# Turning the adjacency matrix of a graph network's second layer from int32 into bf16 during the first layer

## The chip, the cores and the metric

The kernel runs on one core of a Trainium2 chip. The metric is device time in microseconds (us) of one execution. The core's engines are called PE (matrix products), DVE (vector work), ACT (activations and copies), POOL (here almost only indirect DMAs) and SP (here only a queue that issues DMAs). Each runs its own instructions in the order in which they stand in its queue.

## The reference, cut to what matters

Four graph layers follow one another on 3327 nodes with 256 features each. All read one adjacency matrix `adj` of 3327 x 3327 int32, which holds zeros and ones; about 1% of it is ones. Each layer ends in a residual and a layer norm.

```python
def layer0(x, adj):              # score of an edge needs all 256 channels
    s, t = x @ Wsrc.T + bsrc, x @ Wtgt.T + btgt
    score = einsum('ijc,c->ij', leaky_relu(s[:, None, :] + t[None, :, :]), a)
    return softmax(where(adj != 0, score, -inf), 1) @ t
def layer1(x, adj):              # score is a sum of two numbers
    h = x @ W.T
    e = leaky_relu((h @ a1)[:, None] + (h @ a2)[None, :])
    return softmax(where(adj == 0, -1e9, e), 1) @ h
for layer in (layer0, layer1, layer2, layer3):
    x = layernorm(x + layer(x, adj))
```

Layers 2 and 3 are dense like layer 1; layer 3 has four heads, twice.

## The kernel before

Nodes come in 26 tiles of 128 rows (the last has 127).

**Layer 0** (`sparse0`) is sparse. It sorts the rows of four sets of 4, 7, 9 and 6 tiles by degree, makes a list of neighbours for each row and gathers the neighbours' rows from a table in device memory. A piece of this work is a *part*: up to four neighbours of all 128 rows of a tile, 237 parts in all. For a part POOL issues one indirect DMA a neighbour (L926, into buffer `g`), DVE scores it (L946 and L952), and once the scores of the whole tile are known, ACT multiplies each gathered row by its weight (L1028) and PE adds it up (L1031). There are 22 buffers `g`, so the gathers of part q wait until PE is done with part q - 22. The emitting loop at L1370 goes through the parts q in order. At each q it emits the steps that `due[q]` holds, the gathers of part q + 8, and the scoring of part q. Since the whole of layer 0 is under a manual schedule, what is emitted first comes first in each engine's queue. Between the parts, `neighbours` makes the lists of the next set: SP loads 512 KB pieces of `adj` (`adj_i`, three buffers), ACT turns them into bf16 (L553), PE and DVE search them.

`at_step(q, what)` puts a step at part q. Parts 39, 102 and 182 begin the sets 1, 2 and 3. While set 3 runs, layer 1 already does the share of its work that needs only the first 11 tiles (`KNOWN`): `ask_early`, `weigh_early` and `add_early` go through 44 pairs, loading int32 pieces of `adj_t`, the transposed matrix, into `at_f`, and leave bf16 copies of them in `at_d`, a buffer in device memory.

**Layer 1** (`one_head` with `l1`) multiplies, for each block of 4 to 6 target tiles, all 26 source tiles j. For each j it needs a strip of `adj_t`. `ask` loads it as int32 (`at_i`, from a pool of eight buffers with the tag `e`), DVE forms the weights `e` from it (`weigh`, L1728), and PE multiplies (L1845). `adjacent` also makes a bf16 copy on ACT (L1755), in a buffer `at` of a pool of three, and sends it to `at_d` through ACT's queue, for the layers behind.

```python
            if (j, b) not in asked:
                ask(j, b)
            at_i = asked.pop((j, b))
            nc.scalar.copy(at[:pn, :w], at_i[:pn, :w])
            copy_rows(nc.scalar, at_d[j * P : j * P + pn, c0:c1], at[:pn, :w])
            return at_i
```

The blocks of layer 1 (`blocks1`) have 5, 6, 4, 5 and 6 tiles and are worked on in `order1`: tiles 11 to 14 first, then 0 to 4, 5 to 10, 15 to 19, 20 to 25. The first block runs while the last set of layer 0 is normed and projected, a step of that after each j. Its loads of `at_i` are asked for three j ahead. The blocks of the tiles 0 to 10 skip the sources j below 11 and add the early sums (L1854).

**Layers 2 and 3** read strips of `at_d` into the three buffers `at`. Every one of these layers takes its features from tiles `feat` in on-chip memory. A second path (`dense0` and all layers anew, under `tc.If(again > 0)`) is for inputs that the sparse lists can't hold; it isn't taken with these inputs.

Of the kernel before, what the change touches and what calls it, by code (L numbers as in the profile page):

```python
# [8 lines left out]
F32 = mybir.dt.float32  # L9
BF16 = mybir.dt.bfloat16  # L10
I32 = mybir.dt.int32
# [8 lines left out]
P = 128  # L20
BANK = 512
# [11 lines left out]
SETS = (4, 7, 9, 6)  # L33
# [10 lines left out]
ROW = 260  # L44
# [6 lines left out]
def gat_stack(  # L51
# [29 lines left out]
    nc = tc.nc  # L81
    n, dim = x.shape
    nt = -(-n // P)
    kc = dim // P
# [4 lines left out]
    def rows_of(it):  # L89
        return min(P, n - it * P)  # L90
# [14 lines left out]
    at_d = dram.tile([nt * P, n], BF16, name="at_d")  # L105
# [15 lines left out]
    KNOWN = sum(SETS[:-2])  # L121
    blocks1 = []
    for lo, hi in ((0, KNOWN), (KNOWN, EARLY), (EARLY, nt)):
        count = -(-(hi - lo) // 6)
        ends = [lo + (hi - lo) * c // count for c in range(count + 1)]
        blocks1 += [list(range(a, b)) for a, b in zip(ends, ends[1:])]
    order1 = sorted(range(len(blocks1)), key=lambda b: (blocks1[b][0] != KNOWN, b))
    rate1_d = [
# [11 lines left out]
    def copy_rows(engine, dst, src):  # L140

        rows = dst.shape[0]
        whole = rows // 16 * 16
        for lo, hi in ((0, whole), (whole, rows)):
            if lo < hi:
                engine.dma_start(dst[lo:hi], src[lo:hi])
# [90 lines left out]
    blocks = [list(range(f, f + s)) for f, s in zip(firsts, sizes)]  # L237
# [3 lines left out]
    def cols_of(block):  # L241
        return block[0] * P, min(n, (block[-1] + 1) * P)
# [45 lines left out]
    def sparse0(lost):  # L288
        GROUP, TURNS, LEAD, SPREAD = 4, 22, 8, 8
        starts = [sum(SETS[:s]) for s in range(len(SETS))]  # L290
        with ExitStack() as s0:
            find = s0.enter_context(tc.tile_pool(name="s_find", bufs=2))
# [18 lines left out]
            def cuts_of(kt):  # L311

                ends = list(range(0, kt, GROUP)) + [kt]
                if kt % GROUP == 1:
                    ends[-2] -= 1
                return list(zip(ends, ends[1:]))
# [18 lines left out]
                )  # L335
                copy_rows(nc.sync, adj_i[:pn, : hi - lo], adj[it * P : it * P + pn, lo:hi])

            w_tgt = find.tile([P, kc, ROW], F32, name="w_tgt0", bufs=1)
            nc.scalar.dma_start(w_tgt[:, :, :dim], w_tgt_t.rearrange("(c p) f -> p c f", p=P))
            a_row = find.tile([P, dim], F32, name="a_row", bufs=1)  # L340
# [815 lines left out]
            def project_next(it):  # L1156
# [12 lines left out]
                for b, block in enumerate(blocks1):  # L1169
                    if it == block[-1]:  # L1170
# [6 lines left out]
                        nc.scalar.copy(row[:t], m[:t])  # L1177
                        nc.sync.dma_start(rate1_d[b][:, :], row[:t])

            trios = [  # L1180
                list(range(lo, min(lo + 3, block[-1] + 1)))
                for block in blocks1 if block[-1] < KNOWN
# [68 lines left out]
            first = neighbours(0)  # L1251
# [25 lines left out]
            ends, begins = {}, {}  # L1277
# [9 lines left out]
            def at_step(q, what, *args):  # L1287
                due.setdefault(q, []).append(lambda: what(*args))
# [17 lines left out]
            for q, key in ends.items():  # L1306
                count = len(cuts_of(seats[key]))
# [21 lines left out]
            for s in range(len(SETS) - 1):  # L1329
# [16 lines left out]
                at += 1  # L1346
            at_step(at, add_early, len(pairs1) - 1)
            at_step(at + 1, keep_early, len(pairs1) - 1)
            def keep_targets(s):
                lo, hi = starts[s] * P, min(n, (starts[s] + SETS[s]) * P)  # L1350
                copy_rows(nc.sync, own_d[s][: hi - lo, AT_TGT:], table_d[1 + lo : 1 + hi, :])
# [6 lines left out]
            for s in range(1, len(SETS)):  # L1358
                at = begins[s] - LEAD - 2
# [234 lines left out]
    def layers(rs, early=0, rest=None):  # L1594
# [145 lines left out]
            at_i = asked[j, b] = edges.tile([P, wide], I32, tag="e", name="at_i", bufs=8)  # L1740
            copy_rows(nc.sync, at_i[:pn, : c1 - c0], adj_t[j * P : j * P + pn, c0:c1])

        def adjacent(j, b, first=False):

            pn = rows_of(j)
            c0, c1 = cols_of((blocks1 if first else blocks)[b])
            w = c1 - c0
            at = links.tile([P, wide], BF16, tag="at", name="at")
            if not first:
                copy_rows(nc.sync, at[:pn, :w], at_d[j * P : j * P + pn, c0:c1])  # L1750
                return at
            if (j, b) not in asked:
# [68 lines left out]
        def one_head(layer, make, banks_next):  # L1821
# [1 line left out]
            folds, ready, used = [], {}, 0  # L1823

            def fetched(j, b):
                at = adjacent(j, b, layer is l1)
                return at, layer.weigh(j, b, at, 0) if layer.leaky else None

            for turn_b, b in enumerate(layer.order):
                block, first = layer.blocks[b], turn_b == 0  # L1830
# [5 lines left out]
                for j in range(skip, nt):  # L1836
                    pj = rows_of(j)
                    work_until(lambda: layer.feat[j] is not None)
                    at, e = ready.pop(j) if j in ready else fetched(j, b)
                    for s, it in enumerate(block):  # L1840
                        pn = rows_of(it)
                        for part in range(1 if layer.leaky else 3):
                            f = layer.feat[j] if layer.leaky else layer.feat[j][:, part, :]
                            a = e if layer.leaky else at
                            nc.tensor.matmul(  # L1845
                                accs[s][:pn, : dim + 1],
                                a[:pj, s * P : s * P + pn],
                                f[:pj, : dim + 1],
                                start=(j == skip and part == 0),
                                stop=(j == nt - 1 and (layer.leaky or part == 2)),  # L1850
                            )
                    if skip and j == skip + LATER:
                        for acc, y in zip(accs, parts):
                            nc.tensor.matmul(  # L1854
                                acc[:, : dim + 1], ident, y, start=False, stop=False
                            )
                    if layer is l1 and first:
                        work_off(2 if j > 10 else 1)
                        if j + 3 < nt:
                            ask(j + 3, b)  # L1860
                        fetch([j + 3])
                        if j > early and late:
                            l1.load_rates(late.pop(0))
                    elif j >= skip + LATER:
                        work_off()
                    if first and j in make:
                        made.append(make[j]())
                        folds += [(j + 4 + i, step) for i, step in enumerate(made[-1].fold())]
                    while folds and folds[0][0] <= j:
                        folds.pop(0)[1]()  # L1870
# [8 lines left out]
                for s, it in enumerate(block):  # L1879
                    pn = rows_of(it)  # L1880
# [258 lines left out]
        def load_heads(w, a):  # L2139
# [21 lines left out]
        l1 = Layer(  # L2161
            "l1", "f", 1, True, None, rate_d=rate1_d
        )
# [25 lines left out]

        if early:  # L2190
            l1.load_rates(late.pop(0), nc.sync)
        for j in range(3):
            ask(j, order1[0])
        fetch(range(3))
        if rest is not None:
# [109 lines left out]
```

## Time and profile before

| | us |
|---|---|
| median of 5 runs | 2906.27 (2897.23 to 2908.82) |
| the profiled execution: time / span of the core | 2908.21 / 2906.3 |
| PE busy | 2317.1 (80%) |
| DVE busy | 2128.0 (73%) |
| POOL busy | 990.4 (34%) |
| ACT busy | 866.0 (30%) |
| data read / written | 333.91 MB / 47.67 MB |

The profile is of one execution. Busy shares are means over stages that have different limits: POOL is busy from the start to about 1330 us, which is layer 0, and nearly idle after it. Layer 1 lies between about 1349 and 1660 us, layer 2 between 1660 and 1970 us, and layer 3 behind that. Lines of a timeline show the start, the time in us, the engine, the line and the operation; square brackets hold the idle time before it and what ended that. Lines of waits show the total in us, how many waits, and the longest.

### The profile page before, as it was taken

How to read it: one execution, taken by the hardware profiler on the slowest of the kernel's cores; microseconds unless marked ns; L12 is line 12 of the kernel's file. 1: busy time of each engine (PE TensorE's matmuls, PEld its weight loads, DVE VectorE, ACT ScalarE, POOL GpSimd, SP SyncE). 2: the span in 40 equal slices, each digit the busy share in tenths (PEclk: the TensorE clock that was granted, in tenths of full speed). 3: DMA queues.
4: the chain of work that ended last, by engine and by line, in shares of the span. 5: the costliest groups of instructions: out<-in, count | busy, mean ns of one | idle time of the engine just before them, and what ended most of it. 6: DMA issues, size and time to landing. Idle time of an engine off the chain costs nothing.

```text
span 2906.3 us, 47736 instructions
## 1 busy us (share of the span) xinstructions
PE 2317.1 (80%) x16764; PEld 1545.2 (53%) x16764; DVE 2128.0 (73%) x5634; ACT 866.0 (30%) x2441; POOL 990.4 (34%) x1059
## 2 busy tenths in 40 slices
PE   7466667555552665767899999999999999999997
PEld 4234435433442444645778888863656667534332
DVE  7799799968872856655455421158999999899997
ACT  4145445443432533544344211111011110111111
POOL 2676777777777777772000000000000000000000
PEclk9577778767776887889999999999999999999998
DMA  7795665555544457766767533331222222212211
GB/s 244 205 266 149 184 188 158 141 142 148 161 115 110 125 162 192 205 178 167 217 179 206 159 93 107 105 90 45 76 82 61 76 79 66 71 43 63 60 45 49
DMA packets 207558, 378.52 MB, mean 130 GB/s; under 512 B 38410, under 2 KB 148080, under 8 KB 206288
## 3 DMA queue, kind: packets, MB, share of 16 engines
q1 hardware_dynamic: 119416, 186.29, 22.6%
q0 software_dynamic: 50768, 154.31, 19.2%
q10 hardware_dynamic: 37128, 34.79, 3.6%
q8 instruction: 137, 2.24, 0.3%
q14 instruction: 109, 0.89, 0.1%
HBM read 333.91 MB, written 47.67 MB: 131 GB/s over the span
## 4 chain that ended last, share of the span: by engine, by line
PE 57%; DVE 15%; POOL 10%; issue 8%; DMA 7%; ACT 3%; ACTq 0%; SPq 0%; DVEq 0%; POOLq 0%
PE acc L1913 18%; PE acc L1845 14%; PE acc L1921 9%; PE acc L1031 9%; POOL g L926 8%; DMA g<-table_d,lst 3%; DVE y L952 3%; DVE e L1728 3%; PE misc L1653 3%; DVE y L946 2%; DVE cand L589 2%; ACT g L1028 1%; DMA at<-at_d 1%; PE early L1234 1%; DVE cand L599 1%
## 5 line engine op out<-in xcount | busy, mean ns | idle before, releaser
L926 POOL DMA_INDIRECT g<-table_d,lst x894 | 851.9, 953 | 275.9 <-issue 234.8
L1728 DVE SCALAR_TENSOR_TENSOR e<-rate,feat,at 128x896 f32<-128x896 f32 (+4 forms) x832 | 843.4, 1078 | 59.3 <-PE acc L1921 47.8
L1913 PE MATMUL acc<-e,feat 128*32 128x384 f32 (+2 forms) x6656 | 691.4, 514 | 2.9 <-DVE e L1728 1.5
L1031 PE MATMUL acc<-g,ident 128*128 128x256 f32 x1766 | 482.6, 429 | 67.4 <-ACT g L1028 46.3
L1913 PEld LDWEIGHTS acc<-e,feat 128*32 128x32 f32 x6656 | 306.8, 110 | 295.2 <-issue 157.4
L1031 PEld LDWEIGHTS acc<-g,ident 128*128 128x128 f32 x1766 | 376.9, 218 | 156.8 <-ACT g L1028 61.5
L1921 PE MATMUL acc<-e,feat 128*32 128x384 f32 (+3 forms) x3328 | 383.5, 512 | 0.0
L1028 ACT ACTIVATE g<-g,w 128x256 f32<-128x256 f32 x883 | 367.5, 495 | 15.0 <-ACT at L1217 10.6
L946 DVE TENSOR_TENSOR y<-g,minus_ps 128x1028 f32<-128x1028 f32 (+2 forms) x233 | 273.3, 1173 | 113.5 <-DMA g<-table_d,lst 106.7
L952 DVE SCALAR_TENSOR_TENSOR y<-y,a_ps 128x257 f32<-128x257 f32 x894 | 324.6, 419 | 14.5 <-PE a_ps L788 2.2
L1845 PE MATMUL acc<-feat,e 128*128 128x257 f32 (+1 forms) x1110 | 255.6, 386 | 16.9 <-DVE e L1728 13.2
L1845 PE MATMUL acc<-feat,at 128*128 128x257 bf16 (+2 forms) x2028 | 241.1, 276 | 9.8 <-DMA at<-at_d 9.2
L1845 PEld LDWEIGHTS acc<-feat,e 128*128 128x128 f32 (+1 forms) x1110 | 210.5, 192 | 51.8 <-DVE e L1728 15.2
L1921 PEld LDWEIGHTS acc<-e,feat 128*32 128x32 f32 (+1 forms) x3328 | 162.0, 110 | 131.0 <-issue 88.8
L1845 PEld LDWEIGHTS <-at 128*128 128x128 bf16 (+2 forms) x2028 | 200.3, 100 | 45.3 <-DMA at<-at_d 10.2
L563 PE MATMUL v<-code,leads 65*128 65x512 bf16 (+1 forms) x182 | 80.0, 440 | 143.5 <-DVE cand L589 100.3
L589 DVE MAX8 cand<-v 128x8 f32<-128x104 f32 (+2 forms) x858 | 157.6, 259 | 3.0 <-PE v L566 3.0
L1706 POOL DMA_DIRECT2D rate3b_d<-rate_rows x4 | 2.1, 520 | 449.8 <-ACT rate_rows L1705 449.8
L1728 DVE SCALAR_TENSOR_TENSOR e<-rate,feat,at_i 128x640 f32<-128x640 f32 (+4 forms) x108 | 95.8, 899 | 77.2 <-DMA at_i<-in_adj_t_dram 25.9
L1031 PE MATMUL acc<-own_of,ident 128*128 128x256 f32 x52 | 29.0, 659 | 136.7 <-ACT own_of L1028 85.6
L2099 POOL TENSOR_TENSOR rstds<-rstds,minus_half 128x7 f32<-128x7 f32 (+1 forms) x4 | 7.6, 1905 | 382.7 <-DVE rstds L2098 382.7
L261 POOL TENSOR_TENSOR rstds<-rstds,minus_half 128x6 f32<-128x6 f32 (+3 forms) x9 | 12.4, 1381 | 359.1 <-DVE rstds L260 359.1
(259 smaller groups left out, 2075.8 us busy)
## 6 DMA issues: line engine op xcount, KB each, us to landing
adj_i<-in_adj_dram SPq DMA_DIRECT2D x75, 512.0 KB
at<-at_d SPq DMA_DIRECT2D x150, 224.0 KB
at<-at_d SPq DMA_DIRECT2D x75, 192.0 KB
at<-at_d SPq DMA_DIRECT2D x75, 191.8 KB
g<-table_d,lst POOLq DMA_INDIRECT x894, 3.0
at_i<-in_adj_t_dram SPq DMA_DIRECT2D x39, 320.0 KB
at_i<-in_adj_t_dram SPq DMA_DIRECT2D x25, 383.5 KB
at_i<-in_adj_t_dram SPq DMA_DIRECT2D x25, 256.0 KB
```

The lines of the kernel that those rows point to most:

```text
L563: nc.tensor.matmul(v[:, :w], leads[:, b, :], code[:, :w], start=True, stop=False)
L589: nc.vector.max(spread[:, c0 + c, :], view(v[:, :w]))
L926: nc.gpsimd.indirect_dma_start(out=g[:, k - k0, :], out_offset=None, in_=table_d[:, :], in_offset=bass.IndirectOffsetOnAxis(ap=entry["lst" ...
L946: nc.vector.tensor_tensor(y, rows, minus_src[:, None, :].to_broadcast([P, m, dim + 1]), op=ALU.max)
L952: nc.vector.scalar_tensor_tensor(y, y, 1.0, a_ps[:, : dim + 1], op0=ALU.mult, op1=ALU.mult, accum_out=sc)
L1028: nc.scalar.activation(rows, rows, AF.Copy, scale=w[:, k : k + 1])
L1031: nc.tensor.matmul(dst, ident, rows, start=start, stop=stop)
L1653: nc.tensor.matmul(pacc[:pn, : dim + self.extra], ht[:, k, :pn], self.weight[:, k, :], start=(k == 0), stop=(k == kc - 1),)
L1728: nc.vector.scalar_tensor_tensor(e[:pn, : c1 - c0], self.rate[b][:pn, h_of, : c1 - c0], q, at[:pn, : c1 - c0], op0=ALU.max, op1=ALU.mult,)
L1845: nc.tensor.matmul(accs[s][:pn, : dim + 1], a[:pj, s * P : s * P + pn], f[:pj, : dim + 1], start=(j == skip and part == 0), stop=(j == nt ...
L1913: nc.tensor.matmul(accs[x][p][q : q + 32, : hi - lo], f[:pj, at0 : at0 + 32], es[at0 // hd][:pj, lo:hi], start=(j == 0), stop=(j == nt - 1),)
L1921: nc.tensor.matmul(accs[x][pairs][h_of * 32 : (h_of + 1) * 32, : hi - lo], f[:pj, dim + h_of : dim + h_of + 1].to_broadcast([pj, 32]), es[ ...
```

## The change

A new list `shorts` cuts the part of `adj_t` that the early pairs don't cover into 149 pieces of 475 to 480 columns. From part 28 on, `load_whole` loads a piece as int32 through SP into one buffer, and `shorten` copies it into bf16 on ACT, into one other buffer, sends it to `at_d` through SP and asks for the next piece. There is one `shorten` a part, at the parts 29 to 177, behind the other steps of that part. The two buffers are those of `w_tgt0` and `a_row`, which are used at the start of the kernel alone. In layer 1, `adjacent` takes the strip from `at_d` as layers 2 and 3 do; `ask`, the copies on ACT and the writes to `at_d` are left out there, except in the second path. The blocks are cut with the larger one first: 6, 5, 5, 4 and 6 tiles, so that the first block in order is tiles 11 to 15, then 0 to 5, 6 to 10, 16 to 19, 20 to 25.

```diff
-        ends = [lo + (hi - lo) * c // count for c in range(count + 1)]
+        ends = [lo - (lo - hi) * c // count for c in range(count + 1)]
...
+            shorts = []
+            for j in range(nt):
+                lo = KNOWN * P if j < KNOWN else 0
+                count = -(-(n - lo) // BANK)
+                ends = [lo + (n - lo) * c // count for c in range(count + 1)]
+                shorts += [(j, a, b) for a, b in zip(ends, ends[1:])]
+            whole = {}
+
+            def load_whole(m):
+                if m >= len(shorts):
+                    return
+                j, lo, hi = shorts[m]
+                pn = rows_of(j)
+                t = whole[m] = find.tile([P, BANK], I32, tag="w_tgt0", name="at_whole", bufs=1)
+                copy_rows(nc.sync, t[:pn, : hi - lo], adj_t[j * P : j * P + pn, lo:hi])
+
+            def shorten(m):
+                j, lo, hi = shorts[m]
+                pn = rows_of(j)
+                t = whole.pop(m)
+                at = find.tile([P, BANK], BF16, tag="a_row", name="at_short", bufs=1)
+                nc.scalar.copy(at[:pn, : hi - lo], t[:pn, : hi - lo])
+                copy_rows(nc.sync, at_d[j * P : j * P + pn, lo:hi], at[:pn, : hi - lo])
+                load_whole(m + 1)
...
+            at = begins[len(SETS) - 1] - len(shorts) - 4
+            at_step(at - 1, load_whole, 0)
+            for m in range(len(shorts)):
+                at_step(at + m, shorten, m)
...
-        def adjacent(j, b, first=False):
+        def adjacent(j, b, one=False, whole=False):
...
-            if not first:
+            if not (one and whole):
                 copy_rows(nc.sync, at[:pn, :w], at_d[j * P : j * P + pn, c0:c1])
                 return at
...
-                at = adjacent(j, b, layer is l1)
+                at = adjacent(j, b, layer is l1, not early)
...
-                        if j + 3 < nt:
+                        if j + 3 < nt and not early:
                             ask(j + 3, b)
...
-        for j in range(3):
+        for j in () if early else range(3):
             ask(j, order1[0])
```

More of the change, by code (lines that the diff above doesn't have):

```diff
@@ L336, in load @@
                 copy_rows(nc.sync, adj_i[:pn, : hi - lo], adj[it * P : it * P + pn, lo:hi])
-            w_tgt = find.tile([P, kc, ROW], F32, name="w_tgt0", bufs=1)
+            w_tgt = find.tile([P, kc, ROW], F32, tag="w_tgt0", name="w_tgt0", bufs=1)
             nc.scalar.dma_start(w_tgt[:, :, :dim], w_tgt_t.rearrange("(c p) f -> p c f", p=P))
-            a_row = find.tile([P, dim], F32, name="a_row", bufs=1)
+            a_row = find.tile([P, dim], F32, tag="a_row", name="a_row", bufs=1)
             nc.scalar.dma_start(
@@ L1741, in ask @@
             copy_rows(nc.sync, at_i[:pn, : c1 - c0], adj_t[j * P : j * P + pn, c0:c1])
-        def adjacent(j, b, first=False):
+        def adjacent(j, b, one=False, whole=False):
             pn = rows_of(j)
-            c0, c1 = cols_of((blocks1 if first else blocks)[b])
+            c0, c1 = cols_of((blocks1 if one else blocks)[b])
             w = c1 - c0
             at = links.tile([P, wide], BF16, tag="at", name="at")
-            if not first:
+            if not (one and whole):
                 copy_rows(nc.sync, at[:pn, :w], at_d[j * P : j * P + pn, c0:c1])
```

## The prediction

> **What bounds the kernel now.** I read the page's slices first, then busy time by stretch, then the waits of layer 0, then PE's timeline in layer 1. The stretches (length, then busy us and instructions of PE, PEld, DVE, ACT, POOL, then PE's clock, DMA share, GB/s):
>
> ```profile
> 262.00:412.00 150.00, 99.90 (x359) 68.10 (x358) 128.73 (x587) 69.99 (x182) 113.42 (x119) 0.76 0.64 183
> 412.00:562.00 150.00, 92.76 (x346) 69.06 (x345) 146.04 (x564) 77.91 (x206) 114.03 (x120) 0.79 0.54 155
> 862.00:1011.00 149.00, 69.45 (x293) 55.48 (x291) 89.73 (x308) 54.03 (x165) 112.85 (x119) 0.76 0.46 119
> 1349.00:1660.00 311.00, 286.35 (x1304) 242.15 (x1305) 162.04 (x351) 115.02 (x239) 10.20 (x11) 0.98 0.67 198
> ```
>
> In layer 0 POOL issues 119 or 120 DMAs in every 150 us, 1.25 us each, whatever the others do: POOL is the bound. DVE is close to it between 412 and 562 us (97% busy). ACT is half idle. Layer 1 belongs to PE, which sits idle for 311 - 286.35 = 24.65 us.
>
> ```profile
> POOL g L926 <- issue: 218.9, 712, 2.0
> DVE y L946 <- DMA g<-table_d,lst: 102.5, 46, 7.0
> POOL g L926 <- PE acc L1031: 19.8, 60, 1.9
> DVE dots L1142 <- DMA sums_d<-hs,lst: 47.8, 2, 40.1
> ```
>
> These are waits of layer 0 (total, times, longest). POOL hardly waits for anyone. Once DVE stood still for 40.1 us, and POOL went on: the 22 buffers are a cushion. I measured it in the trace, setting each part's first gather beside the end of ACT's scaling of the part 22 places before: 10 to 30 us at parts 61 to 77 (400 to 490 us), 31 us or more behind that.
>
> **Layer 0: what is added.** 149 copies on ACT and 312 DMA issues on SP (149 loads, 149 stores; the seven pieces of the last row tile split in two). A copy of 480 columns lies between these rows, at 0.59 us:
>
> ```profile
> L1217 ACT CAST at<-at_f 128x384 bf16<-128x384 int32 x33 | 16.7, 506 | 24.2 <-DMA at_f<-in_adj_t_dram 22.2 <-ACT part L1242 0.8 <-DMA at_d<-at 0.8
> L1755 ACT CAST at<-at_i 128x512 bf16<-128x512 int32 x25 | 15.5, 619 | 24.2 <-DMA at_d<-at 8.7 <-DMA sums_d<-hs,lst 6.2 <-DMA at_i<-in_adj_t_dram 6.2
> ```
>
> 149 x 0.59 = 88 us fit into ACT, which from 262 to 1011 us has over 400 us idle. The wait matters more. With one buffer, a load is issued only after the copy before it, and the next copy waits for that load; behind it on ACT stand the scaling of the next part (PE and then POOL's buffers wait for that), the `adj_b` copies (PE's search and DVE's scan wait) and `minus_ps` (DVE's scoring waits). So ACT can't go faster than one turn of copy, store issue, load issue, landing. SP is in the turn too: `adj_i`, `xt` and `feats_d`, which now run ahead, stand behind the store of the part before. They still come some two parts before their readers, so I cost them at nothing; with that cover gone each late one would hold ACT or PE by one landing of about 3 us.
>
> The landing, from SP's issue to the start of the copy, by the nearest rows: 128 KB among gathers, and 320 KB in layer 1.
>
> ```profile
> 1134.97 0.33 SPq L146 DMA_DIRECT2D at_f<-in_adj_t_dram  x1
> 1138.02 0.41 ACT L1217 CAST at<-at_f 128x256 bf16<-128x256 int32 x1 [4.33 <-DMA at_f<-in_adj_t_dram]
> ...
> 1420.54 19.12 SPq L146 DMA_DIRECT2D at_i<-in_adj_t_dram  x10
> 1423.63 0.72 ACT L1755 CAST at<-at_i 128x640 bf16<-128x640 int32 x1 [8.50 <-DMA at_i<-in_adj_t_dram]
> ```
>
> 3.05 and 3.09 us. The piece has 245 KB, so 3.1 us at least. The transfers also grow: 36.4 MB in and 18.2 MB out over 749 us are 73 GB/s more, beside 119 to 183; at the rows' 0.64 for 183 GB/s that is 0.26 more share, up to 0.9. For this and for the store ahead in the queue I allow up to 1 us more. A turn: 0.59 + 0.5 (waking SP and the store's issue of 0.33 us, an estimate) + 3.1 to 4.1 = 4.2 to 5.2 us; I take 4.6. Part 29 is scored at 262.4 us and part 178 at 1011.0 us, so POOL needs 749 / 149 = 5.02 us a part. Below that a turn only shifts ACT within the cushion: cost 0 to 6 us, I take 2. A gain is excluded: POOL loses no instruction.
>
> The Trainium skill ("Trainium Kernel Development and Optimization", Best Practices) says to double-buffer so that transfers overlap compute; this speaks against the change. No run here shows the two-buffer case. Followed strictly, copy and landing add up on ACT and layer 0 goes the way of the slow rival below.
>
> The skill's "DMA: Bandwidth & Descriptors" (Anatomy of one DMA) gives 2.0 us plus bytes / 436 GB/s, an estimate of 2.6 us for the piece, measured on another issuing path; the row of 3.05 us for half the bytes differs and decides. By the rule the turn would be 3.7 us and layer 0 free.
>
> **Layer 1: what goes, what comes.** Gone are 113 loads of `at_i`, 108 ACT copies and their stores; strips are half as large. ACT and DMA aren't the bound there, and DVE gains nothing: its weights take 1.0 us with either type at 768 columns.
>
> ```profile
> L1728 DVE SCALAR_TENSOR_TENSOR e<-rate,feat,at 128x768 f32<-128x768 f32 x200 | 189.2, 1009 | 11.5 <-PE acc L1921 10.6
> L1728 DVE SCALAR_TENSOR_TENSOR e<-rate,feat,at_i 128x768 f32<-128x768 f32 x14 | 14.0, 1015 | 13.0 <-DMA at_i<-in_adj_t_dram 6.7 <-PE acc L1845 6.0 <-PE acc L1854 0.3
> ```
>
> The products are the same in number (the larger first blocks only move tiles), so only PE's idle time can shrink:
>
> ```profile
> 1350.08 5.44 PE L1845 MATMUL acc<-feat,e 128*128 128x257 f32 x24 [1.13 <-issue]
> 1357.30 3.92 PE L1845 MATMUL acc<-feat,e 128*128 128x257 f32 x16 [1.78 <-DVE e L1728]
> 1365.71 8.89 PE L1845 MATMUL acc<-feat,e 128*128 128x257 f32 x32 [2.34 <-DVE mv L1090]
> 1418.86 2.15 PE L1845 MATMUL acc<-feat,e 128*128 128x257 f32 x8 [2.66 <-DVE e L1728]
> 1426.03 6.77 PE L1845 MATMUL acc<-feat,e 128*128 128x257 f32 x30 [2.00 <-DVE e L1728]
> 1471.01 4.26 PE L1845 MATMUL acc<-feat,e 128*128 128x257 f32 x11 [3.98 <-DVE e L1728]
> 1354.20 0.62 ACT L1755 CAST at<-at_i 128x512 bf16<-128x512 int32 x1 [6.23 <-DMA sums_d<-hs,lst]
> ```
>
> Block changes cost 2.66 + 2.00 + 3.98, and 0.82 + 1.29 at 1582 to 1590 us, 10.75 together, because `e` waits for int32 strips. With strips of half the size, a longer first block over the next block's rates, and (in the changed DVE order) three weights formed before the change of block, I let 8.5 of it go.
>
> The start gets worse. The first three `at_i` sit in early-free memory, so PE begins layer 1 at 1350.08. The buffer `at` is free only at 1354.20 (last line). A strip asked for then is there at 1357.3 (3.1 us), `e` at 1358.2 (0.88 us, the mean of 128 x 640), so PE stands 1348.9 to 1358.2 = 9.3 us. Before, it stood 5.8 us until 1376 in five pieces (1.13, 1.78, 0.15, 2.34, 0.38): 3.5 us lost. Layer 1: -8.5 + 3.5 = -5.
>
> **Sum.** 2908.2 (profiled execution) + 2 - 5 = 2905; it stands 1.9 us above the median, so 2903.
>
> **Rivals.** *ACT's turn passes POOL's 5.02 us* (slower). All 149 turns then set layer 0's pace, less the cushion of some 34 us. At 5.5 us: 149 x 0.48 - 34 = 38 us, total 2941; it decides from 5.25 us on. For it: DMA share up to 0.9, DVE at 97% with only 10 us of cushion near 450 us. Against: the rows give 4.2 us.
>
> *Layer 1 waits on three buffers `at` instead* (no gain). Layer 2 reads so and pays for it:
>
> ```profile
> L1845 PE MATMUL acc<-feat,at 128*128 128x257 bf16 (+2 forms) x2028 | 241.1, 276 | 9.8 <-DMA at<-at_d 9.2
> ```
>
> 9.2 us in place of 10.75, plus the 3.5 and 2: 2906.3 + 4 = 2910. Against: there PE itself holds the strip, here DVE frees it and eight `e` lie between.
>
> That layer 1 still reads int32 is ruled out by the diff.
>
> **Chances.** 0.3% of 2906 is 8.7 us, about what a measurement can tell. Forecast 0.60: faster past that bound 0.25 (if the start costs nothing or all block waits go), same 0.35. ACT's turn 0.28, slower. Three buffers 0.12: same 0.05, slower 0.07 with some of layer 0's 6 us. Range: all block waits gone and no start cost, 2906.3 - 13 = 2893, rounded to 2890; up to the rival at 5.5 us with its extras, 2945.
>
> **What would show it.** Right: POOL keeps 119 DMAs in 150 us, the copies come 4.6 us or less apart when ACT has no other work, PE idles about 20 us in layer 1, 9 of it before its first product. Wrong: long waits of POOL for PE L1031 before 1011 us, DVE waiting for ACT, or layer 0 ending past 1355 us.

## The result, and the profile after

The changed kernel takes 2909.53 us (median of 33 runs, 2898.57 to 2919.84), the kernel before 2906.03 us (median of 55, 2897.23 to 2914.03). The ratio is 1.0014, with a 95% interval of 1.0007 to 1.002: some 4 us slower, where 3 us less were forecast. The profiled execution of the changed kernel is one of its long ones (span 2920.2 us), a second one took 2900.2 us. What differs between these two is part of the answer. Two of the five sets of runs below fell on chips on which layer 0 of every kernel, that of before too, takes 400 us more (3313.51 and 3316.46 us before); ratios from these sets are marked "3300 us set".

In the lines after, everything behind L1178 has moved: the copies of the pieces are L1201, layer 1's weights are L1758 (L1728 before), its products L1875 (L1845 before). First the busy time by stretch, with the columns of the prediction; the last stretch is layer 1, which now lies 23 us later.

```profile
262.00:412.00 150.00, 95.54 (x312) 63.93 (x310) 119.67 (x545) 70.93 (x177) 110.39 (x116) 0.71 0.74 219
412.00:562.00 150.00, 92.89 (x323) 66.56 (x322) 123.73 (x524) 82.42 (x204) 104.90 (x110) 0.76 0.73 211
862.00:1011.00 149.00, 70.62 (x221) 50.15 (x220) 94.47 (x340) 59.47 (x155) 112.98 (x119) 0.73 0.65 180
1372.00:1683.00 311.00, 291.71 (x1349) 248.98 (x1350) 168.72 (x367) 40.59 (x131) 11.65 (x12) 0.97 0.31 86
```

POOL issues 110 DMAs instead of 120 between 412 and 562 us, while DVE, the engine that was full there, falls from 146 to 124 us. Neither engine is the bound in that stretch any more; something makes both wait. Layer 1 reads half the bytes (86 GB/s, 198 before), and PE is idle for 19.3 us of it, 24.65 before.

The waits of layer 0 (150 to 1340 us; total, times, longest) name it. Before:

```profile
ACT w L990 <- DVE top L985: 182.1, 22, 24.1
...
PE acc L1031 <- ACT g L1028: 45.6, 35, 6.7
```

After:

```profile
ACT at_short L1201 <- DMA at_whole<-in_adj_t_dram: 286.0, 118, 6.1
...
PE acc L1031 <- ACT g L1028: 145.0, 76, 5.7
...
POOL g L926 <- PE acc L1031: 25.8, 39, 12.5
```

ACT stands before 118 of 149 copies and waits for the piece to land. PE's waits for ACT's scaling (L1028) were 45.6 us before and are 145.0. At the end of this chain POOL waits once for 12.5 us; before, its longest wait for PE was 1.9 us. That one wait in the timeline:

```profile
455.01 0.43 SPq L146 DMA_DIRECT2D at_whole<-in_adj_t_dram  x1
...
459.68 0.96 POOL L926 DMA_INDIRECT g<-table_d,lst  x1 [0.30 <-issue]
462.11 0.59 ACT L1201 CAST at_short<-at_whole 128x480 bf16<-128x480 int32 x1 [6.06 <-DMA at_whole<-in_adj_t_dram]
462.73 0.33 SPq L146 DMA_DIRECT2D at_d<-at_short  x1
463.10 0.43 SPq L146 DMA_DIRECT2D at_whole<-in_adj_t_dram  x1
466.37 0.59 ACT L1201 CAST at_short<-at_whole 128x480 bf16<-128x480 int32 x1 [3.38 <-DMA at_whole<-in_adj_t_dram]
...
468.64 3.28 ACT L1028 ACTIVATE g<-g,w 128x256 f32<-128x256 f32 x8
...
469.81 4.81 PE L1031 MATMUL acc<-g,ident 128*128 128x256 f32 x16
...
473.17 0.95 POOL L926 DMA_INDIRECT g<-table_d,lst  x1 [12.53 <-PE acc L1031]
```

The chain reads from top to bottom: a load of 7.1 us (455.01 to 462.11), the copy, store and next load at once behind it, another 3.3 us, only then ACT scales the rows of part 49, PE adds them up, and the buffer that part 71 needs is free 12.5 us late. Part 71 is the place where the cushion (from the end of ACT's scaling of part 49 to the first gather of part 71) was 9.8 us before.

The stages, one profiled execution each (us). Layer 0 is taken from POOL's first gather to PE's last L1031, since the first gather itself moves by some microseconds from execution to execution; layer 1 from there to layer 2's first product.

| | layer 0 | PE's gap before layer 1 | layer 1 | layer 2 |
|---|---|---|---|---|
| before | 1267.6 | 1.1 | 309.1 | 271.8 |
| changed, first | 1287.2 | 9.0 | 304.1 | 267.5 |
| changed, second (again) | 1273.0 | 8.9 | 300.8 | 269.2 |
| l0_only | 1279.3 | 1.1 | 311.6 | 269.2 |
| three_bufs | 1269.1 | 8.7 | 298.4 | 269.2 |
| no_copy_c | 1269.3 | 9.2 | 304.2 | 266.4 |
| load_first_c | 1275.6 | 8.7 | 298.5 | 269.2 |
| copy_twice_c | 1326.6 | 9.9 | 304.9 | 266.4 |
| late | 1346.9 | 8.9 | 298.8 | 268.2 |
| old_cut_c | 1285.4 | 8.5 | 294.5 | 271.3 |
| best_c | 1273.2 | 1.1 | 293.6 | 267.5 |
| best_old | 1278.6 | 1.1 | 289.6 | 267.8 |

Layer 3 took 976.5 to 977.1 us in all of them.

### The profile page after: what moved, and what is told of

It is laid out like the page before. It is cut to its first block, busy times and chain, and to the rows that moved or that the text cites. A ratio compares the mean times of both kernels' runs of the same rounds, so it can differ in the third digit from the quotient of the medians.

```text
span 2920.2 us, 48145 instructions
## 1 busy us (share of the span) xinstructions
PE 2368.2 (81%) x16764; PEld 1575.2 (54%) x16764; DVE 2125.8 (73%) x5634; ACT 873.9 (30%) x2482; POOL 993.1 (34%) x1059
## 4 chain that ended last, share of the span: by engine, by line
PE 55%; DMA 16%; DVE 10%; POOL 6%; issue 6%; ACT 5%; SPq 1%; ACTq 0%; DVEq 0%; POOLq 0%
PE acc L1943 18%; PE acc L1875 15%; DMA at_whole<-in_adj_t_dram 11%; PE acc L1951 9%; PE acc L1031 6%; POOL g L926 6%; PE misc L1683 3%; DVE e L1758 3%; DMA g<-table_d,lst 3%; ACT at_short L1201 2%; DVE y L952 2%; DVE y L946 1%; ACT g L1028 1%; SPq L146 1%; DVE cand L589 1%
## 5 line engine op out<-in xcount | busy, mean ns | idle before, releaser
L1758 DVE SCALAR_TENSOR_TENSOR e<-rate,feat,at 128x896 f32<-128x896 f32 (+5 forms) x940 | 939.6, 1057 | 154.8 <-PE acc L1875 73.9
L1031 PE MATMUL acc<-g,ident 128*128 128x256 f32 x1766 | 532.2, 459 | 171.0 <-ACT g L1028 156.4
L1031 PEld LDWEIGHTS acc<-g,ident 128*128 128x128 f32 x1766 | 396.6, 232 | 297.9 <-ACT g L1028 205.0
L1028 ACT ACTIVATE g<-g,w 128x256 f32<-128x256 f32 x883 | 371.6, 495 | 15.0 <-ACT at L1242 9.3
L1875 PE MATMUL acc<-feat,e 128*128 128x257 f32 (+1 forms) x1110 | 252.5, 385 | 9.6 <-issue 9.0
L1875 PE MATMUL acc<-feat,at 128*128 128x257 bf16 (+2 forms) x2028 | 239.2, 275 | 6.5 <-DMA at<-at_d 6.0
L1875 PEld LDWEIGHTS acc<-feat,e 128*128 128x128 f32 (+1 forms) x1110 | 212.4, 193 | 40.6 <-issue 9.6
L1875 PEld LDWEIGHTS <-at 128*128 128x128 bf16 (+2 forms) x2028 | 199.3, 99 | 40.9 <-DMA at<-at_d 4.8
L1201 ACT CAST at_short<-at_whole 128x475 bf16<-128x475 int32 (+4 forms) x149 | 87.8, 589 | 293.6 <-DMA at_whole<-in_adj_t_dram 286.0
L1798 ACT COPY turned<-misc 128x256 f32<-128x256 f32 (+1 forms) x58 | 21.5, 371 | 383.2 <-PE misc L1795 383.2
```

The source lines that it names most:

```text
L1028: nc.scalar.activation(rows, rows, AF.Copy, scale=w[:, k : k + 1])
L1031: nc.tensor.matmul(dst, ident, rows, start=start, stop=stop)
L1201: nc.scalar.copy(at[:pn, : hi - lo], t[:pn, : hi - lo])
L1758: nc.vector.scalar_tensor_tensor(e[:pn, : c1 - c0], self.rate[b][:pn, h_of, : c1 - c0], q, at[:pn, : c1 - c0], op0=ALU.max, op1=ALU.mult,)
L1875: nc.tensor.matmul(accs[s][:pn, : dim + 1], a[:pj, s * P : s * P + pn], f[:pj, : dim + 1], start=(j == skip and part == 0), stop=(j == nt ...
```

## The experiments

The theory: with one buffer each, a piece costs ACT a whole turn of copy, store, load and landing; the turn is as long as POOL takes for a part (5.02 us by the prediction; the section behind corrects this to 5.12) or longer, so the scaling on ACT falls behind, and the cushion of 22 buffers is too thin at part 71. The rivals: the bytes themselves slow layer 0; or the layer's delay was an accident of one execution.

Times are medians, each with the ratio to the kernel before on the same chip and its 95% interval. Each trace shows one execution only.

**The changed kernel again, and its two halves.**

> The changed kernel as it is, a second execution under the profiler. In the first one layer 0 ended 23 us late (PE's last L1031 at 1371.9 us instead of 1348.9), 12.5 us of it in one wait of POOL for PE L1031 at 473 us. Theory (ACT's turn of 5 us and more uses up the cushion of 10 us that part 71 has): POOL waits over 5 us in all for PE L1031 between 380 and 520 us again, layer 0 ends 5 to 25 us later than before, layer 1 takes 305 us. Rival (the stall was an accident of that one execution, its time was 12 us above the median): no wait over 2 us, layer 0 ends by 1353 us. Time 2909.5 by either.

2909.57 us, 1.0011 (0.9999 to 1.0023). In this execution layer 0 lost 5.4 us instead of 19.6. POOL waited 5.1 us in all for PE between 380 and 520 us, just over what the theory asked for, and its longest wait was 2.3 us, just over what the rival allowed. So the stall's size is an accident, as the rival had it, but its place is not: the cushion of part 71 was 2.8 us in the first, 2.7 in the second execution, against 9.8 before. That is all that is left of it when POOL has to wait, the time for PE to add up part 49. With a single buffer the kernel's runs lie between 2902.01 and 2919.17 us; with three buffers (below) between 2897.44 and 2902.57.

> The additions to layer 0 alone; layer 1 reads int32, copies and writes as before, in its old blocks. Theory (layer 0 costs 8 us in the median, layer 1 gives 5 back): 2906 + 8 = 2914, layer 1 back at 310 us and PE's first gap there below 6 us. Rival (layer 0 costs only what the median shows, 3.5 us, and layer 1 gives nothing): 2909.5.

```diff
-                at = adjacent(j, b, layer is l1, not early)
+                at = adjacent(j, b, layer is l1, True)
...
-                        if j + 3 < nt and not early:
+                        if j + 3 < nt:
```

(and the first three loads and the block sizes as before.) 2922.02 us, 1.0059 (1.004 to 1.0078), 14.5 us above the before of its set. That is 8 us over the theory's 2914: layer 0 costs more than it said, and the rest of the change (the bf16 strips in layer 1 and the new block sizes) is worth 12.5 us (2922.02 to 2909.57).

**Three buffers instead of one.**

> Three buffers for the int32 piece and three for the bf16 piece, in memory of layer 1's inputs that is not written before the end of the third set; a load is asked for three parts ahead. The same bytes, the same copies in the same order on ACT. Theory (the turn on ACT is what costs): ACT's waits for the loaded piece fall from 286 us to under 20, no wait of POOL for PE L1031 over 2 us, layer 0 ends at 1349 to 1353 us, time 2909.5 - 8.5 = 2901. Rival (the 73 GB/s of new traffic slow the gathers and the other loads): layer 0 ends as late as in the changed kernel, 2909.

```diff
-    h = [nodes.tile([P, dim], F32, name=f"h{it}") for it in range(nt)]
+    h_all = nodes.tile([P, nt * dim], F32, name="h_all"); h = [h_all[:, it * dim : (it + 1) * dim] for it in range(nt)]
-                t = whole[m] = find.tile([P, BANK], I32, tag="w_tgt0", name="at_whole", bufs=1)
+                t = whole[m] = h_all[:, (20 + m % 3 * 2) * dim : (22 + m % 3 * 2) * dim].bitcast(I32)
-                at = find.tile([P, BANK], BF16, tag="a_row", name="at_short", bufs=1)
+                at = h_all[:, (17 + m % 3) * dim : (18 + m % 3) * dim].bitcast(BF16)
-                load_whole(m + 1)
+                load_whole(m + 3)
-            at_step(at - 1, load_whole, 0)
+            [at_step(at - 3 + m, load_whole, m) for m in range(3)]
```

2898.95 us, 0.9977 (0.9967 to 0.9986): 10.6 us faster than with one buffer, 2 us below the theory's 2901, and layer 0 is 1.5 us longer than before the change. The cushion at part 71 is 12.1 us. The stretch in which POOL had fallen to 110 DMAs, and the waits of layer 0:

```profile
412.00:562.00 150.00, 92.70 (x345) 67.69 (x343) 143.96 (x558) 94.22 (x239) 114.11 (x120) 0.80 0.79 241
```

```profile
ACT w L990 <- DVE top L985: 165.2, 22, 22.9
...
POOL g L926 <- PE acc L1031: 19.0, 59, 1.3
```

POOL is back at 120, with more bytes in the same time (241 GB/s, 211 with one buffer). ACT waits for DVE's scores again (165.2 us), as it did before the change (182.1), and no longer for pieces. Two buffers were not run.

**The bytes without the copies.**

> The 149 copies on ACT are left out: the loads stay as they are, and the stores send a constant piece of ones, so the layers behind compute with other numbers in the same instructions. The same bytes move; ACT waits for none of them. Theory (ACT's turn is the cost): layer 0 ends at 1349 to 1352 us, the time is that of three buffers or a little less, 2896 to 2900. Rival (the added traffic is the cost): layer 0 ends at 1354 to 1372 us, 2909.

> The 149 copies on ACT left out, all loads and stores kept (the stores send ones, so the layers behind compute with other numbers). Theory (the turn on ACT is the cost, the bytes are not): layer 0 takes 1267 to 1270 us from the first gather to PE's last L1031, as before the change (1267.6) and with three buffers (1269.1); time 2896 to 2900. Rival (the bytes cost a few us): 1273 us and more, 2903 and more.

```diff
-                t = whole.pop(m)
-                at = find.tile([P, BANK], BF16, tag="a_row", name="at_short", bufs=1)
-                nc.scalar.copy(at[:pn, : hi - lo], t[:pn, : hi - lo])
+                whole.pop(m)
+                if m == 0:
+                    whole["at"] = find.tile([P, BANK], BF16, tag="a_row", name="at_short", bufs=1)
+                    nc.vector.memset(whole["at"], 1.0)
+                at = whole["at"]
```

The layers behind then read ones in place of the matrix, in the same instructions. 2901.53 us, 0.9981 (0.9973 to 0.999), in a 3300 us set 0.9948 (0.9921 to 0.9974). Layer 0 takes 1269.3 us, as with three buffers, although 0.84 of the DMA engines' time is taken between 412 and 562 us, and the cushion at part 71 is 9.1 us:

```profile
412.00:562.00 150.00, 93.99 (x368) 70.04 (x367) 143.04 (x561) 79.70 (x212) 114.04 (x120) 0.82 0.84 241
```

Where one buffer costs more than three, it costs through ACT's wait. (The time is 1.5 us over the expected range.) With the bytes alone layer 0 is 1.7 us longer than before, but that is a difference of two things: POOL's last gather comes 7.3 us later than before (6.9 with three buffers), and PE is done 21.3 us after it instead of 26.9. The section behind takes them apart.

**A shorter and a longer turn.**

> One buffer each, but SP issues the next load before the store of the piece, so the turn loses the store's issue, 0.33 us: 4.96 to 5.16 us become 4.6 to 4.8, below POOL's 5.02 us a part. Theory (turn against POOL's pace, with the cushion between): layer 0's cost of 5 to 20 us falls to under 4, PE's last L1031 at 1350 to 1354 us, time 2900 to 2904. Rival (the landing just gets longer, or the turn is not what decides): 2909.

> One buffer each, the next load issued before the store, once more on a chip of the usual pace. Theory (turn against POOL's pace): the turn's median falls from 5.0 to 4.6 or 4.7 us, PE's last L1031 at 1350 to 1354 us, time 2900 to 2904. Rival: 2909.

> One buffer each, the next load issued before the store. Theory (turn against POOL's pace): the turn's median falls from 5.0 to 4.6 or 4.7 us, PE's last L1031 at 1350 to 1354 us, time 2900 to 2904 on a chip of the usual pace. Rival (the turn does not get shorter, since the store now stands behind the load and the buffer of the bf16 piece comes free later): 2909.

```diff
-                copy_rows(nc.sync, at_d[j * P : j * P + pn, lo:hi], at[:pn, : hi - lo])
-                load_whole(m + 1)
+                load_whole(m + 1)
+                copy_rows(nc.sync, at_d[j * P : j * P + pn, lo:hi], at[:pn, : hi - lo])
```

2902.39 us, 0.9992 (0.998 to 1.0005), the time that the theory expected. The turn's median went from 5.04 us (again; the 4.96 of the expectation had counted some waits as copies) to 4.83, 0.21 us less instead of 0.33, because the next wait is already there: the bf16 buffer must be empty.

```profile
ACT at_short L1201 <- DMA at_d<-at_short: 254.0, 112, 5.1
```

By the ratios (1.0014 to 0.9992) swapping two issues took some 6 us off the 10.6 that one buffer costs. The trace doesn't show where: it is of an execution of 2909.18 us, 6.8 over the median, with turns of 5.46 us in the mean (5.45 in again), a longest wait of POOL for PE of 3.2 us, and a layer 0 that ends at 1362.9 us, not at the expected 1350 to 1354. The 3300 us sets gave 0.9991 (0.9967 to 1.0016) and 1.002 (1.0007 to 1.0032).

> Each piece is copied twice in a row on ACT (the second copy writes the same numbers), so that the turn grows by 0.59 us, to 5.6 us, and nothing else changes. Theory (turn against POOL's 5.02 us a part, less a cushion): 149 x 0.59 = 88 us of delay on ACT, of which the cushion holds back some 30 to 40: layer 0 ends 45 to 60 us later than in the changed kernel, time 2955 to 2970. Rival (ACT has over 200 us of idle time left, so 88 us more of work fit in): 2910 to 2915.

> Each piece is copied twice in a row on ACT, the turn grows by 0.59 us and nothing else changes. On the slow chip, where a part of layer 0 took 6.7 us, this cost nothing that could be measured (1.0011). Theory (turn against POOL's pace a part, 5.02 us here, less a cushion): 149 x 0.59 = 88 us of delay on ACT, of which the cushion holds back 30 to 40: layer 0 ends 45 to 60 us later than in the changed kernel, time 2955 to 2970. Rival (it is not the turn's length; 88 us more of work fit into ACT's idle time): 2910 to 2915.

```diff
                 nc.scalar.copy(at[:pn, : hi - lo], t[:pn, : hi - lo])
+                nc.scalar.copy(at[:pn, : hi - lo], t[:pn, : hi - lo])
```

2951.51 us, 1.0152 (1.0127 to 1.0178), 3.5 us below the theory's range. The turn's median is 5.64 us, and in the profiled execution, which took 2959.51 us, layer 0 is 39 to 54 us longer than in the two of the changed kernel.

```profile
ACT at_short L1201 <- DMA at_whole<-in_adj_t_dram: 287.5, 118, 5.0
...
POOL g L926 <- PE acc L1031: 37.3, 49, 17.1
```

ACT waits for the pieces as long as in the changed kernel (287.5 us against 286.0): the 88 us of copies did not go into this idle time, they made each turn longer. That is the answer to "88 us fit into ACT's idle time". Not all of the loss is the cushion of part 71: POOL also waits 17.0 us for DVE's ranks (L692) at the next lists and 9.0 us for DVE's sums (L1052). In a 3300 us set the same kernel gave 1.0011 (0.9992 to 1.003): there a part took about 7 us, and the longer turn cost nothing that could be measured.

**The pieces at other parts.**

> The same single buffers, but the pieces begin at part 81 instead of 29 and end at part 229. From part 81 on the cushion was 31 us or more before the change. Theory (the turn costs only where the cushion is 10 us): turns stay at 5 us, but POOL is not held up, layer 0 ends at 1349 to 1355 us, time 2901 to 2904. Rival 1 (traffic): 2909. Rival 2 (the turn is longer than POOL's 5.02 us a part everywhere, and what is lost adds up until the end, since the last pieces now stand 7 parts before the end of layer 0): layer 0 ends 15 us late or more, 2915.

```diff
-            at = begins[len(SETS) - 1] - len(shorts) - 4
+            at = 81
```

2976.04 us, 1.0229 (1.0205 to 1.0253), by far the slowest, where the theory said 2901 to 2904. The first rival's 2909 fell as well; the second rival's mechanism held, with five times its size. Up to part 200 POOL keeps its pace as expected, and part 71, which now lies ahead of the pieces, has 10.6 us of cushion. The pieces use the cushion up all the same: at part 182 it is 36 us instead of the 52 of before, at part 230 it is 3 instead of 66. From part 182 on the early pairs of layer 1 stand on the same two queues:

```profile
ACT at_short L1201 <- DMA at_whole<-in_adj_t_dram: 134.6, 34, 8.1
DVE e L1246 <- DMA at_f<-feats_d: 105.0, 30, 13.0
```

(waits from 1100 to 1430 us.) Their loads `at_f` stand on SP behind a store that waits for ACT:

```profile
1208.59 0.59 ACT L1201 CAST at_short<-at_whole 128x475 bf16<-128x475 int32 x1 [0.40 <-ACT at L1242]
...
1209.20 0.33 SPq L146 DMA_DIRECT2D at_d<-at_short  x1
...
1210.13 0.40 SPq L146 DMA_DIRECT2D at_f<-in_adj_t_dram  x1
...
1210.58 0.48 SPq L1228 DMA_DIRECT2D at_f<-feats_d  x1
...
1215.37 0.62 DVE L1246 SCALAR_TENSOR_TENSOR e<-rate,at_f 128x384 f32<-128x384 f32 x1 [3.74 <-DMA at_f<-feats_d]
```

So two loops go through one queue, and the mean turn is 6.4 us there (5.6 up to part 182). That this coupling makes it longer is read from these rows; no run takes the two loops apart. PE's last product of layer 0 comes 78 us after POOL's last gather (27 before the change), and as layer 0 ends seven parts after the last piece, nothing of it is made up. In the changed kernel the last piece is at part 177 of 236, and ACT catches up for free: at part 236 the cushion is 53 us, as before. I had counted only POOL's buffers as the cushion; the parts behind the last piece are one, too.

**Layer 1: the block sizes and the start.**

> The changed kernel with the old block sizes 5, 6, 4, 5, 6. Theory (the smaller strips do most, the longer first block a little): PE idles 1 to 3 us more at the changes of block, time 2911. Rival 1 (the cut does nothing): 2909.5. Rival 2 (without the longer first block the block changes wait as long as with int32): 2916.

> The changed kernel with the old block sizes, once more. On the slow chip layer 1 took 294.7 us by this cut and 299 by the new one. Theory 1 (the old cut is as good or better: PE's time in layer 1 is 3 to 4 us less): 2906. Theory 2 (layer 2 starts later by as much, 272.1 us instead of 267): 2909.5. Theory 3 (the longer first block helps): 2912.

> The changed kernel with the old block sizes 5, 6, 4, 5, 6. Theory (the new cut makes layer 1 longer, since the block of five tiles needs a fifth weight column that DVE and the steps of the last set of layer 0 have to share; seen on the slow chips as 294.7 against 298.9 us): 2909.5 - 4 = 2905.5. Rival (what layer 1 gains there, layer 2 loses at its start): 2909.5.

```diff
-        ends = [lo - (lo - hi) * c // count for c in range(count + 1)]
+        ends = [lo + (hi - lo) * c // count for c in range(count + 1)]
```

2910.87 us, 1.0013 (1.0 to 1.0027); in the 3300 us sets 1.0009 (0.9988 to 1.003) and 1.0007 (0.9989 to 1.0026). The changed kernel has 1.0014: the block sizes make no difference here. They move time, though. With the old ones layer 1 takes 294.5 us, 4 to 10 less than with the new ones; PE's pauses in it add up to 15.7 us, against 19.1 in the changed kernel. And PE works for 25.7 us after POOL's last gather, against 21.0 and 21.6 in the changed kernel. Theory and rivals had looked at layer 1 and 2 alone. What in the end of layer 0 depends on the cut was not tested.

> Three buffers in layer 0 as in the run before, and the first block of layer 1 takes its bf16 strips, as the int32 strips were taken, from the pool of eight buffers that is free earlier, three sources ahead. Theory (PE's 8.7 us of idle time before its first product of layer 1 is the wait for the buffer and its load): the gap falls to 1 to 2 us, and with it the slow-clock stretch of 6.8 us that follows; time 2899 - 7.5 - 2 = 2889. Rival (something else is late next, DVE's weights or the features): the gap is only moved behind the first sources, 2895 to 2899.

> Three buffers in layer 0 and the first block's strips from the pool of eight, once more, since the run before fell on a chip on which every kernel, that of before too, took 400 us more in layer 0. There PE's first gap of layer 1 fell from 8.7 to 1.1 us and layer 1 took 290.8 us. Theory: 2907 - 8.5 - 8 = 2890. Rival (the gain of the start is lost again in layer 2, or the buffers' gain was that of one chip): 2897.

> Three buffers in layer 0 and the first block's strips from the pool of eight. Theory, on a chip of the usual pace: 2907 - 8.5 - 8 = 2890, PE's first gap of layer 1 at 1.1 us and layer 1 at 291 us. Rival (the buffers' gain, or the start's, is lost again behind it): 2897.

```diff
+            if early:
+                at_i = asked[j, b] = at_i.bitcast(BF16)
+                copy_rows(nc.sync, at_i[:pn, : c1 - c0], at_d[j * P : j * P + pn, c0:c1])
+                return
...
+            if one and not whole and (j, b) in asked:
+                return asked.pop((j, b))
...
-                        if j + 3 < nt and not early:
+                        if j + 3 < nt:
...
-        for j in () if early else range(3):
+        for j in range(3):
```

With three_bufs' edit beside it. 2891.92 us, 0.995 (0.9932 to 0.9969), in the 3300 us sets 0.9928 (0.9903 to 0.9954) and 0.9945 (0.9925 to 0.9965): the version that beats both. PE's timeline where layer 1 begins (the products are L1881 here):

```profile
1356.23 3.72 PE L1031 MATMUL acc<-g,ident 128*128 128x256 f32 x16 [0.76 <-ACT g L1028]
1361.08 6.74 PE L1881 MATMUL acc<-feat,e 128*128 128x257 f32 x30 [1.13 <-issue]
1368.85 2.40 PE L1881 MATMUL acc<-feat,e 128*128 128x257 f32 x10 [1.02 <-DVE e L1758]
1371.74 4.60 PE L1881 MATMUL acc<-feat,e 128*128 128x257 f32 x20 [0.49 <-DVE e L1758]
```

The gap of 8.7 us is 1.13, and 1.5 us of it come back as waits for DVE's weights.

> Three buffers in layer 0, the first block's strips from the pool of eight, and the old block sizes. Theory (the three gains add up): 2892 - 4 = 2888. Rival (the cut's gain is only that the long pause at the start covered more, and with that pause gone the first block of four tiles waits for its strips or weights as it did with int32): 2892 or more.

2900.03 us, 0.9972 (0.996 to 0.9984): the two gains don't add up, as the rival said. In the profiled executions layer 1 is 4 us shorter than in best_c and layer 0 is 5.4 us longer, 3.4 of it behind POOL's last gather, so the loss does not come from the wait that the rival named, of which there is 2.05 us. The intervals of best_c and best_old overlap.

## Why the prediction was wrong

**The cushion: right; POOL's pace: a little off.** 10 us of cushion at parts 61 to 77 were read from the trace before, and part 71 is where it broke. The pace was read at the wrong rows: 262.4 and 1011.0 us are where parts 28 and 175 are scored; part 29 is scored at 266.8 us and part 178 at 1029.4, which is 5.12 us a part.

**The turn: the step that failed.** "Landing 3.1 to 4.1 ... I take 4.6 ... below that a turn only shifts ACT within the cushion: cost 0 to 6 us, I take 2." The term was too small, and the turn was not below the pace. From load issue to copy it was 4.14 us in the median of the first execution and 4.0 in "again", and over 6.3 and 5.9 in every tenth piece. The turn's median was 5.16 us in the first execution and 5.04 in "again". By these medians ACT would about keep up with 5.12 us a part. Its mean, with the long landings in it, was 5.58 and 5.45, while with three buffers, where the copies can follow the parts, they came 5.24 apart. So ACT fell back by 0.2 to 0.3 us a part. From part 80 on the cushion of before (31 us or more) took that up: at part 134, where before it was 39 us, it was 26 and 25. At part 71 there were 9.8 us, and they were gone. Layer 0 cost 5.4 and 19.6 us in the two profiled executions; by the medians, 10.6 between one buffer and three, and 1.5 that three still cost in their profile, together 12.

**The slow rival** was this mechanism. Its formula gives 149 x 0.62 - 34 = 58 us for layer 0 at copy_twice_c's turn of 5.64 us, and the profiled execution took 59 more than before, but that is luck: with the mean turn, 5.92, and 5.12 a part it gives 85, with the median of the changed kernel nothing, and POOL lost its time at a few places (below), not evenly over 149 turns. Its point of decision was wrong: the cost does not begin at 5.25 us, as 5.04 and 5.16 already cost 10.6.

**A second place** was not in the prediction. While POOL makes the lists of the next set, it waits for its own small DMAs, and these waits grew with the traffic. Before, and in the first execution of the changed kernel:

```profile
POOL lists_d L741 <- DMA lists_d<-payload,ranks_i: 3.4, 3, 1.3
```

```profile
POOL lists_d L741 <- DMA lists_d<-payload,ranks_i: 13.2, 7, 3.0
```

With three buffers it is 7.2 us. How much later than before POOL issues the same gather, counted from its first (us), shows the places side by side; the last column is the time from POOL's last gather to PE's last L1031:

| | behind the lists of set 1 | behind part 71 | behind the lists of set 2 | last gather | PE behind it |
|---|---|---|---|---|---|
| before | 0 | 0 | 0 | 0 | 26.9 |
| changed, first | 4.4 | 16.7 | 22.7 | 25.5 | 21.0 |
| changed, second (again) | 4.3 | 6.2 | 11.5 | 10.7 | 21.6 |
| l0_only | 4.2 | 10.3 | 14.5 | 14.5 | 24.2 |
| load_first_c | 2.5 | 5.6 | 11.7 | 12.6 | 22.3 |
| copy_twice_c | 4.7 | 22.3 | 41.6 | 55.1 | 30.8 |
| three_bufs | 1.8 | 2.2 | 4.6 | 6.9 | 21.5 |
| no_copy_c | 3.3 | 3.5 | 4.8 | 7.3 | 21.3 |
| late | 0.4 | 0.7 | 2.7 | 28.0 | 78.2 |

(Gathers 161, 301, 401 and 898 of 898.) A step at part 71 is there with one buffer alone. A step at the lists is there whatever the buffers, wherever pieces are being moved: late, whose pieces begin at part 81, has none at set 1 and 2 us at set 2. So the new traffic costs POOL some 7 us, which the prediction put at nothing, and an end of layer 0 that is some 5 us shorter hides most of it (PE behind the last gather: 24.2 to 27.1 us with the old block sizes, old_cut_c and best_old included; 21.0 to 23.7 with the new ones, best_c included, but for copy_twice_c and late).

**The Trainium skill's rule of double buffers** ("Trainium Kernel Development and Optimization", Best Practices) was weighed and its price left to the rival. The three_bufs run shows it was right here, with 10.6 us for three buffers. **The formula of "DMA: Bandwidth & Descriptors"** (Anatomy of one DMA) gave an estimate of 2.6 us for a piece; the page fits it to DMAs that GpSimd issues, these are issued by SP. The shortest time from issue to copy in the first execution was 2.78 us, the median 4.14. The measurement decides.

**Layer 1's idle time: right, with some luck, and the gain of layer 1 larger.** PE's pauses from layer 0's last products to layer 2's first, added up, fell from 24.4 to 19.1 us, -5.3 where -5 was forecast, with 8.96 us at the start (9.3 forecast) and single pauses of at most 0.72 us around the block changes:

```profile
1380.83 27.11 PE L1875 MATMUL acc<-feat,e 128*128 128x257 f32 x110 [8.96 <-issue]
...
1456.47 3.71 PE L1875 MATMUL acc<-feat,e 128*128 128x257 f32 x16 [0.59 <-DVE inv L1912]
```

But layer 1 got 5 to 10.7 us shorter, since the products took less time as well: 1110 of them 255.6 us before, 258.2 in l0_only, 252.5, 250.1 and 249.4 in the changed kernel, its second execution and three_bufs. Part of it is the clock. Before, the record shows PE at half its clock for 3.4 us after each of three pauses, in l0_only for 17 us in all, with three buffers once for 6.8 us. So a pause at a block change cost more than its length. But half the clock for 3.4 us more than with three buffers is 2 us of products at most, and in the first execution of the changed kernel PE had half its clock for 20.5 us and its products were still 3 us shorter than before; the rest stays open.

**The longer first block** was counted as a help. In layer 1 it is none: PE's pauses are 15.7 us with the old sizes and 19.1 with the new, so the -5 came out right with this term wrong and the others better than forecast. It is worth nothing in the whole time here. With the start repaired the new sizes look better by 0.2% (0.995 against 0.9972, on two chips), but the intervals overlap (0.9932 to 0.9969 and 0.996 to 0.9984).

**The sum.** +2 - 5 was forecast; about +12 and -8 came out (three_bufs' 0.9977 is 6.7 us, and 1.5 us of layer 0 are in it; l0_only alone puts both higher, at 14.5 and 12.5). Two of the prediction's signs of being wrong came: POOL did wait long for PE L1031, and layer 0 ended past 1355 us in the first execution. The rival of three buffers `at` did not show.

## What to carry to other kernels

A loop of one buffer (load, compute, store, next load) is not "hidden in idle time": the engine that carries it can go no faster than one turn, and everything behind it in its queue takes that pace. Set the turn, with the landing as it is under the new traffic and its long cases, beside the pace of the queue that it shares; if it isn't clearly shorter, give it more buffers before anything else (here three were enough). When reading slack, look for its thinnest place, not its sum, and ask how many steps remain to catch up behind the last use.

## What the runs showed of the hardware

In two sets of runs, on chips that the record numbers 8 and 14, the same kernel before took 3313.51 and 3316.46 us. A later set on a chip numbered 8 took 2906.97 us, so, if the number stands for the same chip, this is no fixed property of it. Layers 1 to 3 were as long as elsewhere, and so was each instruction (a gather's issue 954 ns in "best" against 953 in "again"), but engines stood still in layer 0, once for 65.4 us, for an event that the profile gives no source. One stretch of "again", then of best_b:

```profile
185.00:210.00 25.00, 21.50 (x79) 13.02 (x78) 24.25 (x114) 13.36 (x34) 18.93 (x20) 0.87 0.89 266
```

```profile
185.00:210.00 25.00, 12.81 (x37) 6.76 (x38) 20.14 (x93) 3.79 (x11) 0.00 (x0) 0.50 0.55 153
```

```profile
ACT keys L623 <- remote: 65.4, 1, 65.4
```

What it waited for was not found. In these sets half a microsecond more in the turn cost nothing that could be measured (a part took 7.0 to 7.2 us), while no copies, or three buffers with the start of layer 1 repaired, still gained 0.5 to 0.7%; why they gain there is open, too.

And a load of 245 KB among the gathers took from 2.8 us to the 7.1 us shown above, from issue to the copy that waited for it. The wait of POOL of 12.5 us stands behind the longest of them; in "again", with the same mean turn to within 0.13 us, the longest wait was 2.3 us.
